# A two-layer graph network on one core: h_prime turned through DRAM, edge masks fused in every batch, layer 0 spread over more steps

## The chip, the core and the metric

The kernel runs on one core of one Trainium2 chip. The metric is the device time of one execution in microseconds. A core has five engines with a queue of instructions each: TensorE (PE in the profile, its weight loads PEld), VectorE (DVE), ScalarE (ACT), GpSimd (POOL) and SyncE (SP, which here only issues DMAs). Each queue is executed in order, and engines wait for one another by semaphores.

## The reference

The inputs are `x`, 16 batches of 1024 nodes with 128 features, and a symmetric adjacency matrix of 0 and 1 for each batch. Two layers follow one another, each with a residual and a layer normalisation.

```python
# layer 0
h = einsum('bnf,df->bnd', x, Ww) + Wb
e = einsum('bjl,bkl->bjk', einsum('bjd,dl->bjl', h, A), h)
e = e + swapaxes(e, 1, 2)
attention = softmax(where(adj > 0, e, 0.0), axis=1) * adj
h_prime = relu(einsum('bij,bjk->bik', attention, h))
ic, fc, oc = (sigmoid(h_prime @ w_u + x @ w_x) for the three gates i, f, o)
x = layernorm(x + oc * tanh(ic * h_prime + fc * x))
# layer 1, four heads
h = einsum('bnf,hfd->hbnd', X, conv_w) + conv_b
Ah = tanh(A * einsum('hbni,hij,hbmj->hbnm', h, attn_w, h))
hh = relu(einsum('hbnm,hbmd->hbnd', Ah, h))
x = layernorm(X + relu(relu(mean(hh, axis=0)) + X))
```

Everything is float32.

## The kernel before

Nodes are cut into NB = 8 blocks of 128. Layer 1 of a batch is a loop of 32 steps, four heads (`hd`) by eight blocks (`m`), in `layer1_step`: two score products of 512 columns (L510) into two of the four PSUM banks of the pool `ps_sc`, two VectorE multiplications with the adjacency (L511), a tanh on ScalarE (L512), and, two steps later (`push`, DELAY = 2), two products into the head's sum (L516). A product on float32 data appears as two records of TensorE in the profile. At the end of a batch, in step 31, `head_uT` computes uT of the next batch's first head (L201, emptied by ScalarE at L203), and `rows` its h rows, blocks 0 to 3 in step 31 and 4 to 7 in step 0 (L481, emptied at L484). These, too, use the four banks of `ps_sc`, in turn.

Layer 0 of the next batch is cut into pieces with names of a letter and a number, run between the steps by a table written by hand, `BETWEEN[step]`, and, for the batch after the next, `AHEAD`. The pieces are: L loads xT and the adjacency (eight tiles of 512 KB, all on SP), X loads x, Q and H project, S computes half of the symmetric scores into `R` (L288, L291), T turns a score block so that the other half is filled, A masks (L345, L346, or the fused form L338 with an edge mask made by E on GpSimd, in batch 0 alone) and takes the exponential (L348), B multiplies by the adjacency, scales h (L353, L357) and issues the product of the block before (L365), R takes relu of the sum into `hpT`, P brings it from features by nodes to nodes by features with eight products on TensorE (L384), with three gate columns beside, G computes the gates, and I, O, V, N finish the gated sum and the layer normalisation into `x1`.

A matrix is turned in batches 1 to 15 by `turn` or `turn_score`: VectorE transposes 32x32 blocks into a buffer with the tag "turn" (two buffers), SP writes it to DRAM (L227, L317), waits until this has landed, and reads it back in four strided DMAs (L230, L320). Layer 0 fills steps 0 to 26 of the batch before, `turn_x1` follows in step 27, and the loads L in step 28. `layer1_end` of the batch before runs in steps 2, 5, 7 and 9 (`ENDING`).

Nothing reorders instructions: each engine gets them in the order in which the Python code issues them.

Of the kernel before, what the change touches and what calls it, by code (L numbers as in the profile page):

```python
# [11 lines left out]
F32 = mybir.dt.float32  # L12
BF16 = mybir.dt.bfloat16
AF = mybir.ActivationFunctionType
# [4 lines left out]
P = 128  # L19
# [4 lines left out]
def two_layer_adjacency_kernel(  # L24
# [44 lines left out]
    a_in = consts.tile([P, P], F32, name="a_in")  # L69
    nc.sync.dma_start(a_in, A)  # L70
    ww_in = consts.tile([P, P], F32, name="ww_in")
# [19 lines left out]

    def load_late_weights():
        nc.sync.dma_start(cw_in[0:1], conv_b.rearrange("(o h) d -> o h d", o=1))
        nc.sync.dma_start(cw_in[1:P], conv_w[:, 0 : D - 1, :].rearrange("h f d -> f h d"))
        nc.sync.dma_start(cw_last, conv_w[:, D - 1 : D, :].rearrange("h f d -> f h d"))
        nc.sync.dma_start(aw, attn_w.rearrange("h i j -> i h j"))

# [6 lines left out]
    but_first = consts.tile([1, P], F32, name="but_first")  # L104
# [10 lines left out]
    a_sym = consts.tile([P, P], F32, name="a_sym")  # L115
    s_ww = consts.tile([P, P], F32, name="s_ww")
# [3 lines left out]
    b_wide = consts.tile([P, P], F32, name="b_wide")  # L120
# [98 lines left out]
    Q = 32  # L219

    def turn(dst, src, name):


        t = sb.tile([P, N], F32, tag="turn", name=f"turn_{name}", bufs=2)
        nc.vector.transpose(t.rearrange("p (k d) -> p k d", d=P), src)
        d = dram.tile([P, N], F32, tag="turn", name=f"dram_{name}")
        nc.sync.dma_start(d, t)  # L227
        dv = d.rearrange("(a i) (k c j) -> c i k a j", i=Q, c=P // Q, j=Q)
        for c in range(P // Q):
            nc.sync.dma_start(  # L230
                dst[ts(c, Q)].rearrange("i (k a j) -> i k a j", a=P // Q, j=Q), dv[c]
            )
# [4 lines left out]
    def layer0(b):  # L237
# [7 lines left out]
        def load():  # L245
            t["xT"] = sb.tile([P, N], F32, tag="xT", name=f"xT_{b}")
            nc.sync.dma_start(t["xT"], xT[b])
            adj_t[b] = []
            for j in range(NB):
                a = adjp.tile([P, N], F32, tag="adj", name=f"adj_{b}_{j}")  # L250
                nc.sync.dma_start(a, adjT[b, ts(j, P), :])
                adj_t[b].append(a)
# [44 lines left out]
        def turn_score(j):  # L297


            R, L, w = t["R"], NB - 1 - j, (NB - 1 - j) * P  # L300
            if b == 0:
                for l0 in range(0, L, 4):
                    ls = range(j + 1 + l0, min(j + 5 + l0, NB))
                    ps = small(f"turn0_{j}_{l0}")
                    for i, l in enumerate(ls):
                        nc.tensor.transpose(ps[:, ts(i, P)], R[:, l, j, :], ident)
                    nc.scalar.copy(
                        R[:, j, ls[0] : ls[-1] + 1, :],
                        ps[:, : len(ls) * P].rearrange("p (l d) -> p l d", d=P),
                    )  # L310
                return
            sq = sb.tile([P, N], F32, tag="turn", name=f"turn0_{b}_{j}", bufs=2)
            nc.vector.transpose(  # L313
                sq[:, :w].rearrange("p (l d) -> p l d", d=P), R[:, j + 1 :, j, :]
            )
            d = dram.tile([P, w], F32, tag=f"turn0_{j}", name=f"dram0_{b}_{j}")
            nc.sync.dma_start(d, sq[:, :w])  # L317
            dv = d.rearrange("(a i) (l c j) -> c i l a j", i=Q, c=P // Q, j=Q)
            for c in range(P // Q):
                nc.sync.dma_start(  # L320
                    R[ts(c, Q), j, j + 1 :, :].rearrange("i l (a j) -> i l a j", j=Q),
                    dv[c],
                )

        def find_edges(j):

            m = sb.tile([P, N], BF16, tag="h1", name=f"edge_{b}_{j}", bufs=NB + 1)
            nc.gpsimd.tensor_scalar(m, adj_t[b][j], 0.0, None, ALU.is_gt)
            t["edge", j] = m.rearrange("p (k d) -> p k d", d=P)

        def mask(j):
            s = t["R"][:, :, j, :]
            nmax = sb.tile([P, 1], F32, tag="nmax", name=f"nmax_{b}_{j}", bufs=4)
            if ("edge", j) in t:
                top = -3e38
                for q, ks in enumerate((ts(0, BH), ts(1, BH)) if j == 0 else [slice(NB)]):
                    highest = sb.tile([P, 1], F32, tag="highest", name=f"highest_{b}_{j}_{q}", bufs=4)
                    nc.vector.tensor_tensor_reduce(  # L338
                        s[:, ks], s[:, ks], t["edge", j][:, ks], 1.0, top, ALU.mult, ALU.max, highest
                    )  # L340
                    top = highest
                nc.vector.tensor_scalar_mul(nmax, highest, -1.0)
            else:
                adj = adj_t[b][j].rearrange("p (k d) -> p k d", d=P)
                nc.vector.scalar_tensor_tensor(s, adj, 0.0, s, op0=ALU.is_gt, op1=ALU.mult)  # L345
                nc.vector.tensor_reduce(nmax, s, AX.XY, ALU.max, negate=True)  # L346
            t["z", j] = sb.tile([P, 1], F32, tag="z", name=f"z_{b}_{j}", bufs=4)
            nc.scalar.activation(s, s, AF.Exp, bias=nmax, accum_out=t["z", j])  # L348

        def weigh(j):  # L350

            s = t["R"][:, :, j, :]
            nc.vector.tensor_mul(s, s, adj_t[b][j].rearrange("p (k d) -> p k d", d=P))  # L353
            rz = sb.tile([P, 1], F32, tag="rz", name=f"rz_{b}_{j}", bufs=4)
            nc.vector.reciprocal(rz, t["z", j])  # L355
            t["hz", j] = sb.tile([P, D], F32, tag="hz", name=f"hz_{b}_{j}", bufs=4)
            nc.scalar.mul(t["hz", j], t["h"][:, j, :D], rz)  # L357
            if j:
                back(j - 1)
# [27 lines left out]
        def gates():  # L387

            gate = t["gate"]
            gflat = gate.rearrange("p k g -> p (k g)")  # L390
            nc.vector.tensor_add(gate, t["hp"][:, :, D : D + 3], gate)
            nc.scalar.activation(gflat, gflat, AF.Exp, scale=-1.0)
            nc.vector.tensor_scalar_add(gflat, gflat, 1.0)
            nc.vector.reciprocal(gflat, gflat)  # L394
            t["u"] = sb.tile([P, NB, D], F32, tag="u", name=f"u0_{b}", bufs=1)
            t["x1"] = sb.tile([P, NB, D + 1], F32, tag="x1", name=f"x1_{b}")
            for ks in PARTS:
                nc.gpsimd.tensor_mul(  # L398
                    t["u"][:, ks], t["x"][:, ks],
                    gate[:, ks, 1:2].to_broadcast([P, ks.stop - ks.start, D]),  # L400
                )
            nc.gpsimd.memset(t["x1"][:, :, 0:1], 1.0)

# [21 lines left out]
        def finish(p):  # L425
# [7 lines left out]
            "L": load, "X": load_x, "R": relu,  # L433
            "P": lambda: rows_hp(GROUPS[:-1]), "p": lambda: rows_hp(GROUPS[-1:]),
            "G": gates,
        }
        for i, ks in enumerate(GROUPS):
            pieces[f"H{i}"] = partial(project_h, [ks])
# [7 lines left out]
        for j in range(NB):  # L446
            for name, piece in (("S", score), ("A", mask), ("B", weigh)):
                pieces[f"{name}{j}"] = partial(piece, j)
            if b == 0:
                pieces[f"E{j}"] = partial(find_edges, j)  # L450
            if j + 1 < NB:
                pieces[f"T{j}"] = partial(turn_score, j)
# [10 lines left out]
    def turn_x1(b):  # L463
        if b:
            x1T_t[b] = sb.tile([P, N], F32, tag="x1T", name=f"x1T_{b}")
            turn(x1T_t[b], x1_t[b][:, :, 0:D], f"x1_{b}")
            return
# [25 lines left out]
    def layer1_step(b, hd, m):  # L493
        x1T, h1, uT = x1T_t[b], h1_t[b, m], u_t[b, hd]
        adj = adj_t[b][m]
# [50 lines left out]
    def layer1_end(b):  # L546
        x1 = x1_t[b][:, :, 1 : D + 1]
        y = sb.tile([P, NB, D], F32, tag="u", name=f"y_{b}", bufs=1)
        turn(y.rearrange("p k d -> p (k d)"), sum_t[b].rearrange("p (k d) -> p k d", d=P), f"sum_{b}")
# [8 lines left out]
    def last_end(b, k0, k1):  # L558
# [19 lines left out]
    run(first, "L X")  # L578
    load_late_weights()
    run(second, "L")  # L580
# [8 lines left out]
    run(first, "P p G")  # L589
# [14 lines left out]
    run(second, "T0 T1 T2")  # L604
    rows(0, range(NB))

    BETWEEN = [
        "H0 H1 H2", "S0", "T0 S1", "T1 S2", "T2 A0", "S3 B0", "T3 A1", "S4 B1",  # L610
        "T4 A2", "S5 B2", "T5 A3", "S6 B3", "T6 A4", "S7 B4", "A5", "B5",
        "A6", "B6", "A7", "B7", "X R", "P", "p G", "I0",
        "O0", "V0", "N0", "", "", "", "", "",
    ]
    AHEAD = {28: "L", 31: "Q0 Q1"}
    TURN = 27
    ENDING = (DELAY, DELAY + 3, DELAY + 5, DELAY + 7)
    end, nxt = None, second
    for b in range(B):
        after = layer0(b + 2) if b + 2 < B else {}  # L620
        for step in range(H * NB):
            hd, m = divmod(step, NB)
            layer1_step(b, hd, m)
            if b and step == 0:
# [3 lines left out]
            run(nxt, BETWEEN[step])  # L628
# [64 lines left out]
```

## Time and profile before

| What | Value |
|---|---|
| median of 12 runs | 2448.54 us (2447.22 to 2450.55) |
| the profiled execution | 2447.96 us |
| its span, first to last instruction | 2446.2 us |
| mean granted TensorE clock | 0.999 |
| DMA share of 16 engines, hardware queue of SP | 25.2% |
| adjacency loads, issue to landing | 8.1 us median, 128 of them |
| instructions | 19911 |

The profile is of one execution. A page gives for each engine the busy time and its share of the span, and a chain of waits that is followed back from the last instruction; the groups give, for one line, operation and shape, the number, busy time and mean length. Matmul records overlap, so that prices of TensorE are taken from start to start.

### The profile page before, as it was taken

Reading aid. Unit: us, or ns where it says so; the run is one execution under the profiler, and the core shown is the slowest. Engines: PE = TensorE matmul, PEld = TensorE weight load, DVE = VectorE, ACT = ScalarE, POOL = GpSimd, SP = SyncE. Lnnn points to the kernel's source line nnn. Section 1 sums busy time; section 2 is a strip of 40 time slices with the busy share of each in tenths; the row PEclk is TensorE's granted clock in tenths of the full one; section 3 lists DMA queues with packets and bytes.
Section 4 is the critical chain, followed back from the end, with each engine's and each line's share of the span. In section 5 each row is a group of like instructions: output and inputs, shape, how many; then the busy total and the mean of one; then the engine's idle time right before and its main releaser. Section 6 shows DMA issues by size and latency. Waiting matters only on the chain.

```text
span 2446.2 us, 19911 instructions
## 1 busy us (share of the span) xinstructions
PE 2426.5 (99%) x6175; PEld 1121.2 (46%) x6175; DVE 1586.7 (65%) x3026; ACT 1083.8 (44%) x1522; POOL 137.4 (6%) x102
## 2 busy tenths in 40 slices
PE   8999999999999999999999999999999999999998
PEld 4444444444444444444444444444444444444444
DVE  6665848657586575866658666585765857658454
ACT  6444444344444444434444344444444444444432
POOL 4000000000000000000000000000000000000000
PEclk9999999999999999999999999999999999999999
DMA  4204124051230512404133140332404223042000
GB/s 174 60 10 143 47 95 95 1 148 42 95 95 9 146 35 95 95 17 146 27 105 84 41 128 21 119 71 66 111 13 125 65 95 84 11 134 55 17 26 9
DMA packets 409057, 180.77 MB, mean 74 GB/s; under 512 B 352630, under 2 KB 377078, under 8 KB 408951
## 3 DMA queue, kind: packets, MB, share of 16 engines
q1 hardware_dynamic: 405927, 171.63, 25.2%
q0 software_dynamic: 2160, 7.87, 0.8%
q8 instruction: 49, 0.80, 0.1%
q14 instruction: 57, 0.47, 0.1%
q10 hardware_dynamic: 864, 0.00, 0.0%
HBM read 127.80 MB, written 51.64 MB: 73 GB/s over the span
## 4 chain that ended last, share of the span: by engine, by line
PE 94%; DVE 3%; DMA 2%; SPq 1%; issue 0%; POOL 0%; ACT 0%; POOLq 0%; DVEq 0%; ACTq 0%
PE sc L510 34%; PE acc L516 34%; PE acc L365 9%; PE sc L288 5%; PE pT_u L201 4%; PE pR L481 4%; PE pT_q L201 1%; PE pt L384 1%; PE pR_h L272 1%; DMA xT<-in_xT_dram 1%; SPq L230 1%; DVE R L338 0%; DMA dram_x<-turn_x 0%; DVE st L184 0%; DVE x L192 0%
## 5 line engine op out<-in xcount | busy, mean ns | idle before, releaser
L511 DVE TENSOR_TENSOR s<-sc,adj 128x512 f32<-128x512 f32 x1008 | 671.3, 685 | 623.4 <-PE sc L510 611.7
L510 PE MATMUL sc<-uT,x1T 128*128 128x512 f32 x2048 | 962.0, 592 | 0.0
L516 PE MATMUL acc<-s,h 128*128 128x512 f32 x2016 | 947.3, 592 | 0.0
L512 ACT ACTIVATE s<-s 128x1024 f32<-128x1024 f32 x504 | 532.9, 1057 | 806.1 <-DVE s L511 798.9
L516 PEld LDWEIGHTS acc<-s,h 128*128 128x128 f32 x2016 | 381.7, 190 | 483.5 <-issue 474.4
L510 PEld LDWEIGHTS sc<-uT,x1T 128*128 128x128 f32 x2048 | 385.7, 190 | 468.8 <-issue 421.2
L365 PE MATMUL acc<-R,hz 128*128 128x512 f32 x512 | 241.1, 593 | 2.3 <-ACT hz L357 2.1
L348 ACT ACTIVATE R<-R,nmax 128x1024 f32<-128x1024 f32 x128 | 147.0, 1148 | 206.4 <-DVE nmax L346 181.9
L353 DVE TENSOR_TENSOR R<-R,adj 128x1024 f32<-128x1024 f32 x128 | 156.3, 1221 | 5.7 <-issue 0.3
L346 DVE TENSOR_REDUCE nmax<-R 128x1 f32<-128x1024 f32 x120 | 146.4, 1220 | 4.1
L288 PE MATMUL sc<-xT,qT 128*128 128x512 f32 (+3 forms) x384 | 145.6, 488 | 0.5 <-ACT R L291 0.5
L365 PEld LDWEIGHTS acc<-R,hz 128*128 128x128 f32 x512 | 95.6, 190 | 108.9 <-issue 85.8
L345 DVE SCALAR_TENSOR_TENSOR R<-adj,R 128x1024 f32<-128x1024 f32 x120 | 143.4, 1195 | 0.0
L189 POOL TENSOR_TENSOR rs<-rs,mhalf 128x8 f32<-128x8 f32 (+2 forms) x35 | 65.8, 1881 | 1209.9 <-DVE rs L188 1014.7
L291 ACT ACTIVATE R<-sc,h 128x512 f32<-128x512 f32 (+1 forms) x192 | 109.2, 579 | 38.2 <-PE sc L288 36.8
L201 PE MATMUL pT_u<-x1T,ms 128*128 128x512 f32 x256 | 120.4, 592 | 0.0
L481 PE MATMUL pR<-cw,x1T 128*128 128x512 f32 x256 | 114.9, 592 | 0.0
L357 ACT ACTIVATE hz<-h,rz 128x128 f32<-128x128 f32 x128 | 51.2, 400 | 126.3 <-DVE rz L355 126.2
L288 PEld LDWEIGHTS sc<-xT,qT 128*128 128x128 f32 x384 | 69.9, 191 | 70.2 <-issue 56.7
L484 ACT COPY h<-pR 128x512 f32<-128x512 f32 x128 | 75.0, 586 | 41.7 <-PE pR L481 41.7
L398 POOL TENSOR_TENSOR u<-x,gate 128x1024 f32<-128x1024 f32 (+1 forms) x17 | 30.6, 1799 | 967.9 <-DVE gate L394 967.9
L313 DVE STREAM_TRANSPOSE turn<-R 128x896 f32<-128x896 f32 (+6 forms) x105 | 73.3, 698 | 15.6 <-DMA dram<-turn 13.2
(109 smaller groups left out, 1028.6 us busy)
## 6 DMA issues: line engine op xcount, KB each, us to landing
adj<-in_adjT_dram SPq DMA_DIRECT2D x128, 512.0 KB, 8.1
xT<-in_xT_dram SPq DMA_DIRECT2D x16, 512.0 KB, 4.6
x<-in_x_dram SPq DMA_DIRECT2D x16, 512.0 KB, 4.1
dram_x<-turn_x SPq DMA_DIRECT2D x15, 512.0 KB, 2.6
x1T<-dram_x SPq DMA_DIRECT2D x60, 128.0 KB, 3.3
dram_sum<-turn_sum SPq DMA_DIRECT2D x15, 512.0 KB, 2.6
y<-dram_sum SPq DMA_DIRECT2D x60, 128.0 KB, 3.3
out_dram<-y POOLq DMA_DIRECT2D x15, 512.0 KB, 3.5
```

Of the source, the lines that this page charges most:

```text
L201: nc.tensor.matmul(ps, w, src[:, ts(q, 512)], start=True, stop=True)
L288: nc.tensor.matmul(ps[:, : at - lo], t["qT"][:, ts(j, P)], t["xT"][:, lo:at], start=True, stop=True)
L345: nc.vector.scalar_tensor_tensor(s, adj, 0.0, s, op0=ALU.is_gt, op1=ALU.mult)
L346: nc.vector.tensor_reduce(nmax, s, AX.XY, ALU.max, negate=True)
L348: nc.scalar.activation(s, s, AF.Exp, bias=nmax, accum_out=t["z", j])
L353: nc.vector.tensor_mul(s, s, adj_t[b][j].rearrange("p (k d) -> p k d", d=P))
L365: nc.tensor.matmul(t["acc"][:, ts(q, 512)], t["hz", j], t["R"][:, ts(q, BH), j, :], start=(j == 0), stop=(j == NB - 1),)
L481: nc.tensor.matmul(ps, x1T_t[b][:, ts(k, P)], cw.rearrange("p h d -> p (h d)"), start=True, stop=True)
L510: nc.tensor.matmul(ps, x1T[:, ts(m, P)], uT[:, ts(q, 512)], start=True, stop=True)
L511: nc.vector.tensor_mul(s[:, ts(q, 512)], ps, adj[:, ts(q, 512)])
L512: nc.scalar.activation(s, s, AF.Tanh)
L516: nc.tensor.matmul(acc[:, ts(q, 512)], h1[:, ts(hd, D)], s[:, ts(q, 512)], start=(m == 0), stop=(m == NB - 1),)
```

## The change

P, in batches 1 to 15, no longer uses TensorE: `turn_hp` transposes `hpT` on VectorE and sends it through DRAM. The gate columns that came with it are computed by three GpSimd products of h_prime with broadcast weights `wu_b` (piece Y, three loads more at the start) and three VectorE reductions (F, i, o); the sigmoid is computed in two parts. The fused mask is used in all batches, with edge masks of one byte in two buffers (E in all batches). The adjacency is loaded tile by tile, from batch 2 on by GpSimd's queue. A hop through DRAM leaves its reads in a list, and `land` issues them after the next step's own instructions. The table spreads layer 0 over step 18 of the batch two before to step 24 of the batch before, `turn_x1` moves to step 25, and the end of a batch to steps 2, 6, 12 and 14. Some constants move to tags of the pool `sb`.

```diff
+    hops = deque()
+    def hop(dst, t, name):
+        d = dram.tile(list(t.shape), F32, tag=f"hop_{t.shape[1]}", name=f"dram_{name}")
+        nc.sync.dma_start(d, t)
+        dv = d.rearrange("(a i) (k c j) -> c i k a j", i=Q, c=P // Q, j=Q)
+        def read():
+            for c in range(P // Q):
+                nc.sync.dma_start(
+                    dst[ts(c, Q)].rearrange("i k (a j) -> i k a j", a=P // Q), dv[c]
+                )
+        hops.append(read)
+    def land():
+        while hops:
+            hops.popleft()()
...
+        def load_adj(j):
+            a = adj_t[b, j] = adjp.tile([P, N], F32, tag="adj", name=f"adj_{b}_{j}")
+            (nc.sync if b < 2 else nc.gpsimd).dma_start(a, adjT[b, ts(j, P), :])
...
-            m = sb.tile([P, N], BF16, tag="h1", name=f"edge_{b}_{j}", bufs=NB + 1)
-            nc.gpsimd.tensor_scalar(m, adj_t[b][j], 0.0, None, ALU.is_gt)
+            if b == 0:
+                m = sb.tile([P, N], BF16, tag="h1", name=f"edge_{b}_{j}", bufs=NB + 1)
+            else:
+                m = sb.tile([P, N], U8, tag="edge", name=f"edge_{b}_{j}")
+            nc.gpsimd.tensor_scalar(m, adj_t[b, j], 0.0, None, ALU.is_gt)
...
-                nc.vector.scalar_tensor_tensor(s, adj, 0.0, s, op0=ALU.is_gt, op1=ALU.mult)
-                nc.vector.tensor_reduce(nmax, s, AX.XY, ALU.max, negate=True)
...
+                nc.vector.tensor_tensor_reduce(
+                    s[:, ks], s[:, ks], t["edge", j][:, ks], 1.0, nmax, ALU.mult, ALU.max, top
+                )
...
+        def turn_hp():
+            t["hp"] = sb.tile([P, NB, D], F32, tag="hp", name=f"hp_{b}", bufs=1)
+            hpT = t["hpT"].rearrange("p (k d) -> p k d", d=P)
+            turn(t["hp"], hpT, f"hp_{b}")
+        def weigh_hp():
+            for g in (1, 0, 2):
+                t["hw", g] = sb.tile([P, NB, D], F32, tag="turn", name=f"hw_{b}_{g}", bufs=2)
+                nc.gpsimd.tensor_mul(
+                    t["hw", g], t["hp"], wu_b[:, g : g + 1, :].to_broadcast([P, NB, D])
+                )
+        def sum_hp(g):
+            hw = sb.tile([P, NB, 1], F32, tag="hw", name=f"hws_{b}_{g}")
+            nc.vector.tensor_reduce(hw, t["hw", g], AX.X, ALU.add)
+            gate = t["gate"][:, :, g : g + 1]
+            nc.vector.tensor_add(gate, hw, gate)
...
-    BETWEEN = [
-        "H0 H1 H2", "S0", "T0 S1", "T1 S2", "T2 A0", "S3 B0", "T3 A1", "S4 B1",
-        "T4 A2", "S5 B2", "T5 A3", "S6 B3", "T6 A4", "S7 B4", "A5", "B5",
-        "A6", "B6", "A7", "B7", "X R", "P", "p G", "I0",
-        "O0", "V0", "N0", "", "", "", "", "",
-    ]
-    AHEAD = {28: "L", 31: "Q0 Q1"}
-    TURN = 27
-    ENDING = (DELAY, DELAY + 3, DELAY + 5, DELAY + 7)
+    BETWEEN = {
+        0: "L7 E5 B1 A3 T5 S6", 1: "B2", 2: "E6 A4", 3: "B3 S7 T6", 4: "E7 A5", 5: "B4", 7: "A6",
+        8: "B5", 10: "A7 B6", 11: "B7", 12: "X R", 13: "P", 16: "Y", 18: "F", 19: "i", 20: "o",
+        21: "I0", 22: "O0", 23: "V0", 24: "N0",
+    }
+    AHEAD = {
+        17: "W", 18: "Q0 Q1", 19: "H0 H1 H2", 20: "S0", 21: "T0 S1", 22: "S2", 23: "S3",
+        25: "L0 S4", 26: "L1 T1", 27: "L2 E0 T2", 28: "L3 E1 T3 S5", 29: "L4 A0 E2",
+        30: "L5 A1 E3 T4", 31: "L6 B0 A2 E4",
+    }
+    FIRST = {
+        0: "E1 A0 T3 S4", 1: "E2 B0 A1 T4 S5", 2: "E3 A2 T5 S6", 3: "E4 B1 A3 T6 S7",
+        4: "E5 B2 A4", 5: "E6 B3 A5", 6: "E7 B4 A6", 7: "B5 A7",
+    }
+    TURN = 25
+    ENDING = (DELAY, 6, 12, 14)
...
             layer1_step(b, hd, m)
+            land()
...
-            run(nxt, BETWEEN[step])
+            run(nxt, plan.get(step, ""))
             if step == TURN and b + 1 < B:
                 turn_x1(b + 1)
             run(after, AHEAD.get(step, ""))
```

In the new table W loads xT alone and L0 to L7 load the adjacency; F, i and o compute the gates; FIRST replaces the first steps in batch 0. The lines that follow these calls, with `head_uT` and `rows` in step 31, stay as they were.

## The prediction

> **What bounds the kernel now.** I read the page's busy shares first, then its chain of waits, then the groups by shape, then timelines of one batch (150.9 us, from the first row projection of L481 at 957.07 us to the next batch's at 1107.94).
>
> ```profile
> PE 2426.5 (99%) x6175; PEld 1121.2 (46%) x6175; DVE 1586.7 (65%) x3026; ACT 1083.8 (44%) x1522; POOL 137.4 (6%) x102
> ...
> PE 94%; DVE 3%; DMA 2%; SPq 1%; issue 0%; POOL 0%; ACT 0%; POOLq 0%; DVEq 0%; ACTq 0%
> ```
>
> TensorE is the bound: nothing else holds more than 3% of the chain, so a matmul removed is time removed, and work added to another engine is free until it makes a matmul wait. The next lines, a TensorE timeline of steps 20 to 22 of a batch, price what is removed (columns: start, length, engine, line, what, count).
>
> ```profile
> 1067.90 1.50 PE L384 MATMUL pt<-ident_g,hpT 128*128 128x131 f32 x12
> 1069.24 1.88 PE L510 MATMUL sc<-uT,x1T 128*128 128x512 f32 x4
> 1070.96 1.88 PE L516 MATMUL acc<-s,h 128*128 128x512 f32 x4
> 1072.67 0.61 PE L384 MATMUL pt<-ident_g,hpT 128*128 128x131 f32 x4
> 1073.12 1.88 PE L510 MATMUL sc<-uT,x1T 128*128 128x512 f32 x4
> ```
>
> Lengths overlap, so I use start to start: 1069.24 - 1067.90 = 1.34 us for twelve records and 1073.12 - 1072.67 = 0.45 for four: 1.79 us a batch, 0.112 a record. A group of four 512-wide records (one layer-1 product over both halves) takes 1070.96 - 1069.24 = 1.72 us; a plain layer-1 step is two such groups, 3.43 us.
>
> The turn of a batch (step 31 and what follows) matters most:
>
> ```profile
> 1102.30 1.88 PE L516 MATMUL acc<-s,h 128*128 128x512 f32 x4
> 1103.29 1.06 ACT L512 ACTIVATE s<-s 128x1024 f32<-128x1024 f32 x1 [2.38 <-DVE s L511]
> 1104.44 1.96 PE L201 MATMUL pT_q<-xT,q_w 128*128 128x512 f32 x4 [0.25 <-DMA xT<-in_xT_dram]
> 1106.23 1.88 PE L201 MATMUL pT_u<-x1T,ms 128*128 128x512 f32 x4
> 1107.29 0.59 ACT L203 COPY uT<-pT_u 128x512 f32<-128x512 f32 x1 [0.17 <-PE pT_u L201]
> 1107.94 3.60 PE L481 MATMUL pR<-cw,x1T 128*128 128x512 f32 x8
> ```
>
> Two things: TensorE waits for xT here, because SP issues xT only behind the x1 turn; and ScalarE empties uT 0.17 us after its product, so the row projections, which reuse the four score banks in turn, never wait.
>
> [...] in batch 0 the fused mask beside the edge work on POOL takes 1.99 us, and 1.21 after it.
>
> ```profile
> 31.88 1.98 DVE L338 CUSTOM_DVE_ANT_0 R<-R,edge 128x1024 f32<-128x1024 f32 x1
> 33.90 0.15 DVE L342 TENSOR_SCALAR nmax<-highest 128x1 f32<-128x1 f32 x1
> 33.98 1.23 DVE L353 TENSOR_TENSOR R<-R,adj 128x1024 f32<-128x1024 f32 x1
> 35.20 1.21 DVE L338 CUSTOM_DVE_ANT_0 R<-R,edge 128x1024 f32<-128x1024 f32 x1
> ```
>
> But L353[...] takes 1.23 either way; [...] +0.8 on the mask. [...] eight of these loads now take SP 4.63 us (1100.06).
>
> **Part by part.**
> 1. *Matmuls removed.* P becomes one VectorE transpose and a trip through DRAM in 15 of 16 batches: 15 x 1.79 = -26.9 us. Batch 0 keeps them.
> 2. *xT earlier.* W is issued at step 17 with nothing ahead of it on SP but the finished h_prime reads; Q moves to step 18. The five visible waits (0.42, 1.51, 0.42, 0.99 and 0.42 us, start to start over 1.72, at 199, 801, 1104, 1555 and 1857 us) go: -3.8 us.
> 3. *VectorE.* The mask falls from 1195 + 1220 ns (L345, L346) to 1.21 + 0.08 + 0.15, or 2.2 beside edge work: 8 x 0.2 to 1.0 us less a batch. New: one 1.24 us transpose, three reductions of about 1.22 (L346's row, same elements) and small gate rows, about 5.8 us. Near zero on an engine busy for 99.41 us of the 150.70 from 1104.00 on; nothing on the path.
> 4. *POOL.* Eight edge masks of 2.8 to 3.35 us (24.31 for 8; one-byte output is not in the trace: bounds 2 to 5, I take 3), eight load issues near 0.97 (L556), three products near 1.90 (L398): about 38 us a batch on an engine now at 7. An edge mask is issued when the mask two before it is done and needed about two steps, 7 us, later. Nothing.
> 5. *h_prime's turn.* From relu at step 12: transpose about 1 step later, 2.6 us write, 4 reads (2.75 us of issue, 3.3 to landing), so it is in SBUF about 9 us after step 13 begins; POOL needs it at step 16, 10 us after. Behind POOL's product stands only the gate chain of steps 18 to 24, with steps to spare. Nothing.
> 6. *Masks moved across the batch turn; the cost I see.* In step 31 the instruction lists place layer 0's B0 and A2 ahead of uT and the row projections. ScalarE executes in order: tanh, hz of B0, the exponential of A2, only then the uT copies. Let s be the start of step 31's first product. VectorE's L511 pair ends at s + 2.6 (1103.20 - 1100.59); B0 1.2 (33.98 to 35.20); A2 1.4 (35.20 to 36.60): s + 5.2. Exponential 1.26 (1148 + 186 ns, overlapping): s + 6.5; uT copy 0.59 and a handover: s + 7.2. TensorE has by then done scores, acc, uT and two rows, 3 x 1.72 + 2 x 0.86 = s + 6.9; its third row projection takes the bank of uT's first half. It waits at least 0.3 us. If the mask of step 30 meets edge work, VectorE reaches L511 0.3 us late, and A2 may itself take up to 0.7 more. I take 0.9 (0.3 to 1.9). Batches 0 to 13 have this: 14 x 0.9 = +12.6 us.
> 7. *SP and turn buffers.* A hop now costs SP 6.5 us (write 983.73, next write 990.27: landing 3.7, four reads 2.7). Reads "a step behind" still stand between write n and write n+1, so a backlogged SP keeps this rate, and steps 25 to 28 post x1, T1, T2, T3 at 3.43 us a step. With two turn buffers, T3's transpose waits until T1's write has landed. I get: x1 transposed at 6.0 us after step 25 begins, landed 8.7, reads issued by 11.5, T1 written by 15.1 to 15.6 under the adjacency loads; VectorE reaches T3 at 13.8. It stands 1.5 us, just the slack that it has before step 29's scores. I count nothing, and it is the weakest zero here.
> 8. *Batch 0.* Masks start at step 0 with less TensorE work per step: 0 to 2 us, I take 1.
>
> Sum against the profiled execution, 2447.96 us (span 2446.2 and 1.8 around it): -26.9 - 3.8 + 12.6 + 1 = -17.1, 2430.9. The median of the runs, 2448.54, is 0.6 higher: forecast 2431 us.
>
> **Rivals.**
> A. *The exponential does not delay uT* (VectorE has the slack after all): -26.9 - 3.8, about 2418. For it: VectorE is at 65%. Against: s + 7.2 already assumes a punctual VectorE. Chance 0.15.
> B. *The forecast*, 0.3 to 1.9 us a batch: 2422 to 2445. Chance 0.53.
> C. *The wait eats the gain*: about 2.2 us a batch, 2444 to 2453. Chance 0.12.
> D. *Slower, by the hop chain of part 7.* From T3 to A2 of step 31 VectorE has no idle time, so every microsecond that T1's write lands later, past the slack, reaches the uT copy and the third row projection one for one. The trace never shows a hop beside adjacency loads; if x1 lands 1.0 and T1 1.9 us later, less 0.5 of slack, the wait is 0.9 + 2.4 = 3.3 us: 14 x 3.3 = 46 - 30.7 + 1 = +16, about 2465. It decides from 2.2 us a batch. For it: SP is serial and the loads move 4 MB in that stretch. Against: one 512 KB load a step keeps the DMA engines part busy only (mean share 0.27 over a batch). Chance 0.20.
>
> **How the numbers follow.** A change within 0.2% (4.9 us) can't be told from none by this measurement. A, B and a tenth of C are faster by more: 0.70; most of C is the same: 0.09; D and C's rest slower: 0.21. The range 2418 to 2457 runs from A to the point where D's upper half is left out.
>
> **What would show it.** No L384 group beyond batch 0, and about 240 TensorE records fewer; no wait of pT_q for xT; row projections with idle time put down to the uT copy, 14 times, near 0.9 us; VectorE's share near 66%, POOL's near 30%. I am wrong if that wait is absent or several microseconds long, if T3's transpose waits over 2 us for its buffer and step 29's scores come late, or if acc or scores wait for masks anywhere else.

## The result, and the profile after

The changed kernel takes 2474.30 us (median of 7 runs, 2473.16 to 2481.97) against 2448.48 (29 runs, 2446.65 to 2451.98): a ratio of 1.0114, 95% interval 1.0104 to 1.0123. It is slower by about 26 us; the forecast was 2431. The profiled execution is the slowest of these, 2481.97 us with a span of 2479.9, which is 33.7 more than the span before; sums over its trace are a few us larger than those of the median run would be.

The page of the changed kernel (busy time by engine, shares of the chain of waits by engine, and one group with its busy time, the mean ns of one, the idle time before it and what ended that):

```profile
PE 2423.9 (98%) x5935; PEld 1099.1 (44%) x5935; DVE 1577.2 (64%) x3266; ACT 1068.7 (43%) x1492; POOL 628.5 (25%) x379
PE 88%; DMA 5%; DVE 4%; ACT 1%; SPq 1%; issue 1%; POOL 0%; DVEq 0%; POOLq 0%; ACTq 0%
L332 DVE STREAM_TRANSPOSE turn<-R 128x896 f32<-128x896 f32 (+6 forms) x105 | 73.6, 701 | 88.9 <-DMA dram_turn<-turn 88.5
```

The 240 matmul records are gone, as promised (6175 to 5935). But TensorE's share of the chain fell from 94% to 88%, and DMA and VectorE rose from 5% to 9% together: something off the bound now reaches it. The waits view of the same kernel (who waited at which line for whom: us in total, times, longest) names a pair:

```profile
DVE turn L332 <- DMA dram_turn<-turn: 88.5, 20, 7.2
PE pR L528 <- ACT uT L209: 34.6, 13, 3.0
PE pT_q L207 <- DMA xT<-in_xT_dram: 2.4, 1, 2.4
```

VectorE waits up to 7.2 us for a turn buffer to be written out, and in almost every batch the row projections then wait some 3 us for uT. One batch's turn shows how one becomes the other. Step 25 begins at 1413.70. SyncE's timeline (start, length, queue, line, what; the length here is the time that SyncE needs to issue):

```profile
1419.81 0.33 SPq L232 DMA_DIRECT2D dram_x<-turn_x  x1
1422.43 3.38 SPq L237 DMA_DIRECT2D x1T<-dram_x  x4
1425.91 2.60 SPq L232 DMA_DIRECT2D dram_turn<-turn  x1
1434.20 2.67 SPq L237 DMA_DIRECT2D R<-dram_turn  x4
```

x1's write lands in 2.62 us (1419.81 to 1422.43, where the first read is issued). The next, T1's write of only 384 KB, starts behind x1's four reads, takes SyncE 2.60 us to issue where x1's 512 KB took 0.33, and has landed only at 1434.20, 8.29 us later. VectorE's timeline of the same stretch:

```profile
1434.23 0.71 DVE L332 STREAM_TRANSPOSE turn<-R 128x512 f32<-128x512 f32 x1 [6.76 <-DMA dram_turn<-turn]
...
1440.39 1.25 DVE L558 TENSOR_TENSOR s<-sc,adj 128x512 f32<-128x512 f32 x2
1442.84 1.20 DVE L350 CUSTOM_DVE_ANT_0 R<-R,edge 128x1024 f32<-128x1024 f32 x1
```

T3's transpose (L332) stands 6.76 us, with every later VectorE instruction behind it; the multiplication of step 31 (1440.39) and A2's mask (1442.84) come late. ScalarE and TensorE, from their timelines:

```profile
1435.81 1.88 PE L557 MATMUL sc<-uT,x1T 128*128 128x512 f32 x4
1441.10 1.98 PE L528 MATMUL pR<-cw,x1T 128*128 128x512 f32 x4
1445.42 1.05 ACT L209 COPY uT<-pT_u 128x512 f32<-128x512 f32 x2
1446.04 3.57 PE L528 MATMUL pR<-cw,x1T 128*128 128x512 f32 x4 [2.95 <-ACT uT L209]
1449.44 1.88 PE L557 MATMUL sc<-uT,x1T 128*128 128x512 f32 x4
```

The uT copies, whose product was done by 1441.1, where the row projections begin, stand behind A2's exponential (L357, 1444.27 to 1445.42), the third row projection behind the first copy: 2.95 us idle. Then comes a second loss. The four records from 1446.04 take 3.40 us to the next group at 1449.44 instead of 1.72. The windows view (stretch, its us, busy time of PE, PEld, DVE, ACT and POOL, granted TensorE clock, share of the DMA engines, GB/s) shows why. The share sums the packets' own times, so that it can pass 1:

```profile
1418.00:1435.00 17.00, 17.00 (x42) 7.65 (x41) 8.12 (x13) 4.44 (x5) 7.19 (x5) 1.00 0.75 207
1442.43:1445.84 3.41, 0.65 (x2) 0.00 (x0) 1.77 (x5) 2.33 (x5) 3.30 (x3) 1.00 1.21 253
1445.84:1449.26 3.42, 3.23 (x4) 1.51 (x5) 0.00 (x0) 2.19 (x5) 1.62 (x2) 0.50 0.81 246
```

The granted clock, 1.00 in the two stretches above, is 0.50 for the 3.42 us in which TensorE restarts, and a record takes 0.85 us instead of 0.43. Between batches the trace has 11 such stretches at a clock of 0.50, of 3.41 us each. Twelve of the 13 waits for uT are 2.47 to 2.95 us long, and a stretch at half speed follows 11 of these. The length of the wait alone does not say which (TensorE's timeline):

```profile
1906.27 3.45 PE L528 MATMUL pR<-cw,x1T 128*128 128x512 f32 x4 [2.47 <-ACT uT L209]
2208.23 1.98 PE L528 MATMUL pR<-cw,x1T 128*128 128x512 f32 x4 [2.54 <-ACT uT L209]
```

Behind the shortest of the 12, 2.47 us, the four records take 3.45 us; behind one of 2.54 they take 1.98, full speed. What decides is not shown.

Over the whole trace, start to start above each form's median, TensorE loses 77.4 us after and 17.1 before:

| Time beyond the medians, us | before | after |
|---|---|---|
| up to the first layer-1 step | 10.1 | 14.1 |
| row projections waiting for uT | 0 | 36.9 |
| half-speed records behind them | 0 | 17.4 |
| all else (3.8 of xT waits in it before) | 7.0 | 9.0 |

77.4 - 17.1 = 60.3 lost, less the 26.9 of removed matmuls, is +33.4; the spans differ by 33.7.

### The profile page after: what moved, and what is told of

Same layout as the page of the kernel before. It is cut to its first block, busy times and chain, and to the rows that moved or that the text cites. A ratio compares the mean times of both kernels' runs of the same rounds, so it can differ in the third digit from the quotient of the medians.

```text
span 2479.9 us, 20210 instructions
## 1 busy us (share of the span) xinstructions
PE 2423.9 (98%) x5935; PEld 1099.1 (44%) x5935; DVE 1577.2 (64%) x3266; ACT 1068.7 (43%) x1492; POOL 628.5 (25%) x379
## 4 chain that ended last, share of the span: by engine, by line
PE 88%; DMA 5%; DVE 4%; ACT 1%; SPq 1%; issue 1%; POOL 0%; DVEq 0%; POOLq 0%; ACTq 0%
PE sc L557 33%; PE acc L563 32%; PE acc L374 9%; PE pR L528 4%; PE sc L307 4%; DMA dram_turn<-turn 4%; PE pT_u L207 4%; DVE s L558 1%; PE pT_q L207 1%; DVE R L350 1%; PE pR_h L291 1%; ACT R L357 1%; DVE R L362 1%; SPq L99 1%; DMA adj<-in_adjT_dram 0%
## 5 line engine op out<-in xcount | busy, mean ns | idle before, releaser
L558 DVE TENSOR_TENSOR s<-sc,adj 128x512 f32<-128x512 f32 x1008 | 681.6, 687 | 681.5 <-PE sc L557 667.3
L343 POOL TENSOR_SCALAR edge<-adj 128x1024 uint8<-128x1024 f32 (+1 forms) x128 | 357.2, 2792 | 469.1 <-DVE top_None L350 456.7
L195 POOL TENSOR_TENSOR rs<-rs,mhalf 128x8 f32<-128x8 f32 (+2 forms) x35 | 54.6, 1561 | 974.1 <-DVE rs L194 974.1
L357 ACT ACTIVATE R<-R,nmax 128x1024 f32<-128x1024 f32 x128 | 146.9, 1148 | 53.7 <-DVE nmax L355 51.7
L528 PE MATMUL pR<-cw,x1T 128*128 128x512 f32 x256 | 135.1, 667 | 35.6 <-ACT uT L209 34.6
L350 DVE CUSTOM_DVE_ANT_0 R<-R,edge 128x1024 f32<-128x1024 f32 (+1 forms) x128 | 154.0, 1203 | 2.9 <-PE turn L325 2.9
L405 POOL TENSOR_TENSOR hw<-hp,wu_b 128x1024 f32<-128x1024 f32 x45 | 106.7, 2383 | 145.1 <-DMA hp<-dram_hp 51.4
L332 DVE STREAM_TRANSPOSE turn<-R 128x896 f32<-128x896 f32 (+6 forms) x105 | 73.6, 701 | 88.9 <-DMA dram_turn<-turn 88.5
L528 PEld LDWEIGHTS pR<-cw,x1T 128*128 128x128 f32 x256 | 50.6, 205 | 108.6 <-ACT uT L209 49.3
L581 DVE SCALAR_TENSOR_TENSOR sum<-acc,sum 128x512 f32<-128x512 f32 x95 | 61.3, 686 | 49.9 <-PE acc L563 49.9
## 6 DMA issues: line engine op xcount, KB each, us to landing
adj<-in_adjT_dram SPq DMA_DIRECT2D x16, 512.0 KB, 10.1
```

The source lines that it names most:

```text
L343: nc.gpsimd.tensor_scalar(m, adj_t[b, j], 0.0, None, ALU.is_gt)
L350: nc.vector.tensor_tensor_reduce(s[:, ks], s[:, ks], t["edge", j][:, ks], 1.0, nmax, ALU.mult, ALU.max, top)
L528: nc.tensor.matmul(ps, x1T_t[b][:, ts(k, P)], cw.rearrange("p h d -> p (h d)"), start=True, stop=True)
L558: nc.vector.tensor_mul(s[:, ts(q, 512)], ps, adj[:, ts(q, 512)])
```

## The experiments

Two causes have to be told apart at the end of the chain (the place of the uT copy behind A2's exponential) and several at its start (x1's reads ahead of T1's write, the adjacency loads beside it, the queue that issues these). In the diffs `-` is the changed kernel. The kernel before had a median near 2446 us in all these sessions.

**e1_ut_first: the uT copy first.** In step 31 `head_uT` and the rows are put ahead of the `AHEAD` pieces.

```diff
+            if step == H * NB - 1 and b + 1 < B:
+                head_uT(b + 1, 0)
+                rows(b + 1, range(NB // 2))
             run(after, AHEAD.get(step, ""))
-            if hd == H - 1 and b + 1 < B:
-                if m == NB - 1:
-                    head_uT(b + 1, 0)
-                    rows(b + 1, range(NB // 2))
-            elif hd < H - 1 and m == NB - 4:
+            if hd < H - 1 and m == NB - 4:
                 head_uT(b, hd + 1)
```

> Step 31 issues head_uT and the four row projections ahead of L6 B0 A2 E4; nothing else changes. Theory: VectorE is late (T3's transpose waits 6.8 us for its buffer), and this reaches TensorE only through ScalarE's order, exponential before uT copy. Then the wait of the third row projection for uT (36.9 us in the profiled execution of the changed kernel) goes, and with it the TensorE records at 0.85 instead of 0.43 us behind it (17.4 us); T3's wait stays at 6 to 8 us. Time 2415 to 2430 us. Rival 1: a VectorE late by 6.8 us stalls TensorE anyway; the wait moves to scores or acc of step 0 and the time stays above 2455. Rival 2: the half-speed records have another cause and stay; time about 2440.

Measured: 2425.48 us, ratio to the kernel before 0.9918 (0.9903 to 0.9932), granted clock 0.999. A line of its waits, then one of TensorE's timeline and two of ScalarE's:

```profile
DVE turn L332 <- DMA dram_turn<-turn: 76.0, 18, 6.5
```

```profile
1404.22 3.74 PE L528 MATMUL pR<-cw,x1T 128*128 128x512 f32 x8
1405.35 1.05 ACT L209 COPY uT<-pT_u 128x512 f32<-128x512 f32 x2
1408.78 1.14 ACT L357 ACTIVATE R<-R,nmax 128x1024 f32<-128x1024 f32 x1
```

VectorE still waits for the turn buffer, 76.0 us in all, yet with the uT copies ahead of the exponential (L357) TensorE's eight row records run without a gap and at full speed; its wait for uT is down to 0.2 us in the whole run. So the late hop costs little by itself (2.9 us more than e3 below, where it is on time): it costs through ScalarE's order, in which uT stood behind A2. The half-speed records went with the wait, which shows that they were its consequence.

**e2_turn27: x1 turned in step 27 again.**

```diff
-    TURN = 25
+    TURN = 27
```

> x1 turned in step 27 as in the kernel before, all else as in the changed kernel. Theory: T1's write lands late (8.2 us) because it runs beside x1's 128-byte reads; with x1 behind it, it lands in 3 to 4 us, T3's wait falls under 1 us and the wait of the row projections to 0.3 to 1.5 us a batch, unless x1T itself comes late for uT. Time 2425 to 2440 us. Rival: the adjacency loads alone make T1 late; T1's landing stays over 6 us and the time above 2465.

Measured: 2496.93 us, ratio 1.0208 (1.0190 to 1.0226). Slower still: the theory fails. The rival's time came true, but not its landing, for T1's write, now with no reads just ahead of it, lands in 5.02 us. SyncE's timeline and a line of the waits:

```profile
1432.10 0.59 SPq L232 DMA_DIRECT2D dram_x<-turn_x  x1
...
1438.33 2.86 SPq L237 DMA_DIRECT2D x1T<-dram_x  x4
```

```profile
DVE turn L332 <- DMA dram_x<-turn_x: 98.1, 14, 7.4
```

Now x1's own write needs 6.23 us (1432.10 to 1438.33), and T3 waits for that. The reads ahead of it are those of a score block, so x1's reads are not the cause in particular: here the write that falls behind T1's reads is late; and turning x1 two steps sooner was itself a gain, 2497 to 2474.

**e3_write_first: the write of the new hop issued ahead of the reads of the hop before.**

```diff
             layer1_step(b, hd, m)
-            land()
+            late = list(hops)
+            hops.clear()
...
             run(after, AHEAD.get(step, ""))
+            for read in late:
+                read()
```

> In each step the write of the new hop is issued ahead of the reads of the hop before. Theory of SP's order: T1's write then starts about 3.5 us sooner, lands before T3's transpose is due, T3's wait falls under 2 us, and the row projections wait 0.3 to 1.5 us a batch: 2425 to 2440 us. Rival, the DMA engines are the limit: T1 still lands over 6 us after its issue and the time moves by less than 10 us.

Measured: 2422.57 us, ratio 0.9904 (0.9887 to 0.9920). Its timelines of SyncE, VectorE and ScalarE:

```profile
1384.53 0.33 SPq L232 DMA_DIRECT2D dram_turn<-turn  x1
1385.11 5.09 SPq L237 DMA_DIRECT2D x1T<-dram_x  x4
...
1390.06 0.70 DVE L332 STREAM_TRANSPOSE turn<-R 128x512 f32<-128x512 f32 x1
1392.74 1.48 DVE L558 TENSOR_TENSOR s<-sc,adj 128x512 f32<-128x512 f32 x2 [1.98 <-PE sc L557]
...
1396.17 1.48 DVE L558 TENSOR_TENSOR s<-sc,adj 128x512 f32<-128x512 f32 x2 [0.63 <-PE sc L557]
...
1404.79 1.05 ACT L209 COPY uT<-pT_u 128x512 f32<-128x512 f32 x2
```

T1's write (1384.53) now goes out 2.05 us after x1's, with no read between them, and lands 4.8 to 5.2 us after its issue in the batches where the trace tells its landing; T3's transpose finds its buffer free, and the delay moves to the x1 reads (5.09 us of issue), which nobody is waiting for. With a punctual T3 the uT copy starts at 1404.79, 6.31 us after step 31's first product (1398.48), and no row projection waits, where 0.3 to 1.5 us a batch were expected.

**e5_no_adj: no adjacency traffic.** Batches 2 to 15 use the adjacency tiles of the batch two before, so 112 loads of 512 KB are left out; the output is that of another adjacency.

```diff
         def load_adj(j):
+            if b > 1:
+                adj_t[b, j] = adj_t[b - 2, j]
+                return
```

> Batches 2 to 15 load no adjacency: they use the tiles of the batch two before, so the 112 loads of 512 KB are left out and nothing else. Theory A, T1's write is late because it shares the DMA engines with the adjacency loads: it lands in 3 to 4 us, T3's wait falls under 1 us, the row projections wait 0.3 to 1.5 us a batch and the time is 2425 to 2440 us. Theory B, the four reads of x1 in 128-byte pieces ahead of it on SP's queue are enough: T1 still lands after 6 us or more and the time stays above 2460.

Measured: 2422.77 us, ratio 0.9906 (0.9891 to 0.9921). SyncE's timeline (the order is that of the changed kernel), and the wait at the transpose:

```profile
1389.94 0.65 SPq L232 DMA_DIRECT2D dram_turn<-turn  x1
1393.23 2.67 SPq L237 DMA_DIRECT2D R<-dram_turn  x4
```

```profile
DVE turn L335 <- DMA dram_turn<-turn: 29.1, 15, 2.6
```

The same write, at the same place behind x1's reads, takes 0.65 us to issue and 3.29 to land instead of 2.60 and 8.29; over the batches from the second on it lands in 3.2 to 4.1 us, and in 5.1 to 8.5 in the changed kernel. T3 waits at most 2.6 us, which is inside VectorE's slack. So the loads account for some 5 us of the landing in the batch shown, and it takes both, the loads and the reads ahead on the queue, to make the wait.

**e9_adj_sp: all adjacency loads issued on SP.** This asks whether the queue that issues them matters.

```diff
-            (nc.sync if b < 2 else nc.gpsimd).dma_start(a, adjT[b, ts(j, P), :])
+            nc.sync.dma_start(a, adjT[b, ts(j, P), :])
```

> All adjacency loads are issued by SP again, at the same steps as in the changed kernel, so that they stand in one queue with the hops. Theory: what makes T1's write late is the traffic on the shared DMA engines, not who issues it; T1's write lands late all the same (over 5 us after its issue, or is issued later by the loads ahead of it), T3's wait stays over 3 us and the time stays above 2460. Rival: it is the second queue[...]; in one queue T1's write waits for its predecessors alone, lands within 4 us of its issue, and the time falls under 2435.

Measured: 2498.44 us, ratio 1.0211 (1.0194 to 1.0228). SyncE's timeline and a line of the waits:

```profile
1430.90 0.38 SPq L232 DMA_DIRECT2D dram_turn<-turn  x1
1436.66 2.67 SPq L237 DMA_DIRECT2D R<-dram_turn  x4
```

```profile
PE pR L528 <- ACT uT L209: 40.2, 14, 2.9
```

T1's write still needs 5.76 us, and rows wait 14 times (13 in the changed kernel). Counted from the start of step 25, T1 has landed after 18.7 us here, 20.5 in the changed kernel and 15.5 in e5. The transposes wait for a buffer 29 times instead of 20, and edge masks now wait for loads as well, 444.7 us in all. This run and e5 point the same way: the write comes in too late whichever queue issues the loads (after 18.7 and 20.5 us), and soon enough without them (15.5).

**e4_wu_late: the three broadcast loads of the gate weights (`wu_b`) behind the second batch's loads.** This is about the start of the kernel.

```diff
-        for g, w in enumerate((wi_u, wf_u, wo_u)):
-            nc.sync.dma_start(wu_b[:, g, :], w.partition_broadcast(P))
...
     run(second, "W L0 L1 L2 L3 L4 L5 L6 L7")
+    for g, w in enumerate((wi_u, wf_u, wo_u)):
+        nc.sync.dma_start(wu_b[:, g, :], w.partition_broadcast(P))
```

> The three broadcast loads of wu_b come behind the second batch's loads instead of ahead of them. Theory: they hold SP for 14 us at the start, which makes the second batch's xT late by 2.6 us and the first layer-1 step start at 74.0 instead of 69.9 us; moved, that start is back at 70 to 71 us and the time falls by 3 to 4 us, to about 2470. Rival: the start is late for the masks of batch 0, which are the same; no change.

Measured: 2461.01 us, ratio 1.0064 (1.0038 to 1.0089). The wait of pT_q for xT, 2.4 us in the table of waits above, is gone, and the first layer-1 step starts at 72.07 us instead of 73.99 (before the change: 69.93). That is worth 1.9 us, not 13. The 14 us for which SyncE is held are not these loads': they belong to the load of `cw_last` ahead of them (L99, 14.15 us of issue), which took 14.29 in the kernel before too; the three broadcasts take SyncE 1.4 us. The rest came from the row projections, which waited 26.4 us in all (12 times) instead of 34.6 (13 times), with 7 half-speed stretches behind them instead of 11. Why those waits shrank is not shown; the runs spread over 15 us (2454.79 to 2470.26). For the turn of the batch this run settles nothing.

**e6_both and e8_both_p: the edits of e1, e3 and e4 together, and the same with P on TensorE again.** The second undoes the main part of the change in an otherwise healthy kernel:

```diff
-        if b == 0:
-            pieces.update(P=lambda: rows_hp(GROUPS), G=gates)
-        else:
-            pieces.update(P=turn_hp, Y=weigh_hp, F=gate_f, i=gate_i, o=gates_io)
+        pieces.update(P=lambda: rows_hp(GROUPS), G=gates)
...
-        8: "B5", 10: "A7 B6", 11: "B7", 12: "X R", 13: "P", 16: "Y", 18: "F", 19: "i", 20: "o",
+        8: "B5", 10: "A7 B6", 11: "B7", 12: "X R", 13: "P", 16: "Y", 18: "G", 19: "i", 20: "o",
```

> Writes ahead of reads, uT and its rows ahead of the masks in step 31, and wu_b loaded behind the second batch's inputs, together. Theory: each of the first two already removes the waits of step 31, so together they add under 3 us; the late wu_b gives back 2 to 4 us at the start: 2416 to 2421 us. Rival: what is left is the start of the kernel and wu_b is not it; 2421 to 2425.

> As e6_both, but h_prime's rows come from TensorE in all batches again (P with gate columns, G at step 18; turn_hp, Y, F, i, o are gone). Theory: with the waits of step 31 away, the 16 records of a batch cost their 1.79 us in full: 26.9 us more than e6_both, 2443 to 2448. Rival: part of them lies where TensorE would wait anyway; under 15 us more.

Measured: e6 takes 2418.65 us (2418.23 to 2418.66), ratio 0.9888 (0.9871 to 0.9904), faster than the kernel before and the changed one; e8 2445.02 (12 runs, 2444.42 to 2447.00), ratio 0.9997 (0.9989 to 1.0006). The difference, 26.4 us, is what P through DRAM is worth. The chain's shares on e6's page:

```profile
PE 97%; SPq 1%; DMA 1%; DVE 1%; issue 0%; ACT 0%; POOL 0%; POOLq 0%; ACTq 0%; DVEq 0%
```

TensorE holds 97% of the chain here; it loses 14.4 us beyond the medians in all (before: 17.1), nearly all of it at the start and the end.

**e7_u8_first: one-byte edge masks in batch 0 too.** A side question. In the changed kernel the fused masks of batch 0 took 1.20 us beside the edge work, where the kernel before had 1.98. Is it the masks' type?

```diff
             if b == 0:
-                m = sb.tile([P, N], BF16, tag="h1", name=f"edge_{b}_{j}", bufs=NB + 1)
+                m = sb.tile([P, N], U8, tag="h1", name=f"edge_{b}_{j}", bufs=NB + 1)
```

> The edge masks of batch 0 have one byte as in the other batches, instead of bf16. Theory: the fused mask is slowed beside GpSimd's edge work by the mask's type, since in steady batches with one byte it takes 1.2 us also beside it; then batch 0's masks fall from 1.99 to about 1.21 us. Rival: it is the overlap itself in batch 0, and they stay near 1.99 us. The whole time moves by less than its run-to-run spread either way, 2470 to 2482.

Measured: 2471.35 us (2 runs), ratio 1.0104, no difference from the changed kernel; masks 1.20 us. But the changed kernel with its two-byte masks has 1.20 as well, and e3, whose batch 0 is the same code as there, 1.98 (VectorE's timelines, first the changed kernel, then e3, each with the multiplication that follows the mask):

```profile
28.22 1.20 DVE L350 CUSTOM_DVE_ANT_0 R<-R,edge 128x1024 f32<-128x1024 f32 x1
...
29.55 1.85 DVE L362 TENSOR_TENSOR R<-R,adj 128x1024 f32<-128x1024 f32 x1
```

```profile
29.02 1.98 DVE L350 CUSTOM_DVE_ANT_0 R<-R,edge 128x1024 f32<-128x1024 f32 x1
...
31.12 1.22 DVE L362 TENSOR_TENSOR R<-R,adj 128x1024 f32<-128x1024 f32 x1
```

So the type is not the cause, and the time has not gone: in the changed kernel the multiplication with the adjacency is the long one, 1.85 us instead of 1.22. In both runs five or four of them are long in batch 0, and each long one lies wholly inside one edge instruction of GpSimd (in the changed kernel the multiplication from 29.55 to 31.40 us inside the one from 28.85 to 32.05), where the short one beside it reaches over the border of two. What lengthens it is not shown, and why neither is long in the steady batches, where some lie inside an edge instruction too (at most 1.29 us), was not found.

## Why the prediction was wrong

The forecast named the chain in its rival D and gave it one chance in five; D's time, 2465, is 9 us short of the median. Step by step:

1. *Matmuls removed, -26.9.* Held: 240 records fewer, and 26.4 us between e8 and e6.
2. *xT sooner, -3.8.* Held in the batches: the five waits are gone. One of 2.4 us in batch 0 is new, because three loads for `wu_b` stand ahead of that xT.
3. *VectorE* and 4. *POOL, nothing.* Held: 64% and 25% busy, and e6 has TensorE at 97% of the chain with the same masks, edges and products (2.79 us an edge mask, 3 assumed). One reading beside it was wrong: the 0.8 us more beside edge work were put on the fused mask alone, since L353 took 1.23 us either way; in the changed kernel that multiplication was the long one, 1.85 us, and the mask took 1.20 (e7).
5. *h_prime's turn, nothing.* Held: no matmul waits for it in e6.
6. *Masks across the batch turn, 0.9 a batch.* ScalarE's order is the way by which lateness reaches TensorE (e1 removes it), and the part's clock held: with a punctual T3, in e3, the uT copy starts 6.31 us after step 31's first product, 6.5 forecast. But its 12.6 us were not there: the first half of uT is copied by about 1405.38, the third row projection, two products after 1403.63, is due at about 1405.35, and by itself the order makes no wait of note. In the changed kernel the copy starts at 9.61 (1435.81 to 1445.42): the lateness came from part 7.
7. *SP and turn buffers, "I count nothing".* **This is the step that failed.** Its times were right up to T1's write. From step 25's start x1's write was issued at 6.1 us (6.0 forecast for its transpose), landed at 8.7 (8.7), its reads were issued by 12.1 (11.5). Then T1 was to be written "by 15.1 to 15.6", 3.6 to 4.1 us after those reads; it landed at 20.5, 8.4 after them. T3's wait became 6.76 instead of 1.5. That estimate took hops measured where no load runs and added too little for loads: without them, in e5, T1 has landed at 15.5, within the forecast, so that the missing term is some 5 us. Part 7 called itself the weakest zero and priced it at zero all the same.
8. *Batch 0, +1.* TensorE lost 4.0 us more than before up to the first layer-1 step; about 1.9 of this is `wu_b`'s place (e4).

Rival D's account was right in mechanism and wrong in two sizes that partly offset each other, which is luck. T1 came far later than the 1.9 us it allowed, but the delay does not reach uT one for one: in e3 VectorE idles 1.98 and 0.63 us between T3 and step 31, and its three multiplications take 1.25 instead of 1.48 once their inputs wait for them. 6.76 - 2.61 - 0.69 leaves 3.5, and the third row projection came 3.4 late. Against that D had no term for the restart: the wait summed to 36.9 us (46 in D), and half speed behind it added 17.4.

Rival A, that ScalarE's order makes no wait, was the truth of the kernel without the late hop: e3, which keeps that order, has no such wait at 2422.57, and its 2418 is what e6 measured, where the start is mended too.

Not tried: a third turn buffer, which would let T3 go ahead of T1's landing. The clock halved after 11 of the 12 waits of 2.47 to 2.95 us in the changed kernel; in e2, with 14 waits of up to 2.9 us, its mean was 0.996, against 0.991 in the changed kernel. Why it halves after one wait and not after another remains open.

## What to carry to other kernels

When a serial queue does write, wait, read for several transfers, price each write at what it takes beside the traffic that will run at that moment (here 8.29 us to land beside the loads, 3.29 without them), and issue the next write ahead of the reads that nobody is waiting for. Where work is moved across the turn of a loop, look at what it is put ahead of in each in-order queue: here one copy of 0.6 us behind an exponential turned a late buffer on VectorE into idle time on the bounding engine. A wait of TensorE of some 3 us should be priced with its restart: here 17.4 us over 11 restarts, 1.6 for each, and none behind a wait of 2.54 us.

## What the runs showed of the hardware

- Beside the loads, issuing took longer as well as landing: behind the same reads, the same DMA instruction took SyncE 0.65 us to issue without the loads and 2.60 beside them, ahead of the longer landing (3.29 and 8.29 us); beside the loads but with no reads ahead, in e3, it took 0.33.
- Busier DMA engines did no harm by themselves: e3 ran with DMA engines busier than the changed kernel in the same steps (share 1.01 over 17 us of these steps, 0.75 there) and lost nothing, because the late transfers were those with slack.
- In the changed kernel the granted TensorE clock fell to 0.50 behind 11 of 12 waits of 2.47 to 2.95 us, for 3.41 us each time, in which a record took 0.85 us instead of 0.43. A wait of 2.47 us cost such a restart and one of 2.54 none; what decides was not found.
- In batch 0, where GpSimd's edge instructions follow one another (3.2 to 3.4 us each), one of two VectorE instructions of a block is longer than in the steady batches: the fused mask (1.98 us instead of 1.20, in e3) or the multiplication (1.85 instead of 1.22, in the changed kernel). In the steady batches neither is long beside edge work (at most 1.29). The cause is not shown.
